# A scratch write behind every row gather in a four-layer graph attention kernel: 320 columns behind each, in place of 256 behind every second

## Chip, cores and metric

The kernel runs on one core of one Trainium2 chip. The metric is the device time of one execution in microseconds. The core's engines are TensorE (PE, with its weight loads shown apart as PEld), VectorE (DVE), ScalarE (ACT), GpSimd (POOL) and SyncE (SP, which issues DMAs).

## What is computed

Four graph attention layers over N = 4096 nodes with 256 features share one adjacency matrix. Each layer normalizes its input, attends along the edges and adds the result to its input:

```
h = maximum(layernorm(x), 0)            # before each layer
x = x + gat_l(h, adj)                   # l = 0..3

# gat_l: h' = h @ W;  s = h' @ a1;  d = h' @ a2
e    = leaky_relu(s[:, None] + d[None, :], 0.2)
attn = softmax(where(adj > 0, e, -big), axis=1)
out  = attn @ h'                        # elu behind it in layers 1 and 3
```

Layer 2 has four heads of 64 columns. Layer 3 has a second attention with -e, and multiplies both results by one matrix. The adjacency is random, and an edge (i, j) is likelier where i and j are small: the first rows are dense, the later ones sparse.

## The kernel before

The nodes are cut into 32 tiles of 128. Blocks of four tiles at the front are computed **densely**: every source tile j is weighed against a 128x512 block of targets (DVE L1151 makes the weights s_p from the target row s_grow, the source's column and the mask) and multiplied on PE (L1193; in layer 2 L1228 and L1210) into accumulators in PSUM. There are 4, 2, 1 and 1 dense blocks in layers 0 to 3. All other target tiles are computed **from lists**. For each of them, the sources that have an edge into it are collected once, in layer 0, in index lists (made with one-hot matmuls L968 and read out into idx at L978). A listed tile T takes the first four source tiles whole, and the others by gathers with an indirect DMA: one gather brings 128 rows of the layer's table in DRAM, named by a column of idx. There are SHARED[T] gathers of rows for the whole tile (s_gg), and QUADS[T] groups of four gathers (s_gq), each of the four for 32 of the targets. That makes 5 to 12 gathers for a tile. In a gathered tile the weights come from L1151 (s_gg) or L1107 and L1110 (s_gq), and L1193 or L1130 multiply them. Where the mask of a tile stands in the same table row, an ACT copy (L1174 for s_gg, L1084 for s_gq) takes it out into mlist for the later layers; masks of the other blocks are gathered in layer 0 by gathers of their own (mlist<-mask_t).

All gathers go through one helper, `gather` (L532), on GpSimd. Behind every second one the helper writes zeros into a scratch tile named pause (L541), which nothing reads. A counter, gathers[0], and the constant RUN = 2 choose after which. GpSimd's order is written out by hand: the whole program of the four layers stands in a manual schedule for that engine, so that what GpSimd does is in the order in which the source emits it. The other engines' orders are set by the framework's scheduler, which reckons with each engine's time. GpSimd's other work is in layer 0: normalization (L732), a bias (L736) and constants.

The order of the work as a whole comes from one plan, a list of steps (unit, i), where a unit is a dense block or a listed tile. `run` goes through it with four stages that stand apart by LEAD = (0, 2, 3, 6) steps: fetch, begin, weigh, multiply. `fetch` is what issues the gathers, six steps ahead of the matmuls that use them. In layer 0 the listed steps are mixed into the later dense blocks; in layers 1 to 3 the dense steps are dealt out over the listed tiles: over 24 tiles in layer 1, over the first 14 in layer 2, and over 26 in layer 3.

The buffers: s_gg has four in layer 0 and six later, s_gq two. A gather waits until the matmuls or weights that used its buffer have run. SP's queue carries the plain loads and stores: the raw adjacency (s_raw<-in_adjT, 128 loads of 512 KB, turned into masks by DVE L1472) in layer 0, the tables' stores, and the streams s_gs and s_ms for the dense blocks.

In time order, layer 0 lasts to about 500 us, layer 1 to about 768, layer 2 to about 1165 and layer 3 to the end. Between layers, GpSimd's first gather waits until the table is complete or a dense start has run: in the trace 58.5 us before layer 1 (the flag that ends layer 0, L1015), 43.1 us before layer 2 (PE L1228) and 30.3 us before layer 3 (the table's store).

Of the kernel before, what the change touches and what calls it, by code (L numbers as in the profile page):

```python
# [8 lines left out]
F32 = mybir.dt.float32  # L9
# [9 lines left out]
P = 128  # L19
# [460 lines left out]
FRONT = tuple(MW * ((l, False) in MASKS_IN.values()) for l in range(4))  # L480
TW = tuple(FRONT[l] + GW[l] + MW * ((l, True) in MASKS_IN.values()) for l in range(4))
LEAD = (0, 2, 3, 6)
RUN = 2
OWN0 = 7
HW = MW // 2
TURNS = (4, 5, 6, 1, 7, 2, 3)
# [3 lines left out]
def list_layers(ctx: ExitStack, tc: tile.TileContext, a: dict, out: bass.AP, flag):  # L490

    nc = tc.nc

    const = ctx.enter_context(tc.tile_pool(name="s_const", bufs=1))
# [29 lines left out]
        nc.gpsimd.memset(places[:, T - TS0 : T - TS0 + 1], float(2 * BASE + P * SHARED[T]))  # L524


    pause = const.tile([P, 256], F32, name="pause")
    gathers = [0]

    def gather(dst, src, index_ap, offset):  # L530

        nc.gpsimd.indirect_dma_start(  # L532
            out=dst,
            out_offset=None,
            in_=src,
            in_offset=bass.IndirectOffsetOnAxis(ap=index_ap, axis=0),
            element_offset=offset,
        )
        gathers[0] += 1
        if gathers[0] % RUN == 0:  # L540
            nc.gpsimd.memset(pause, 0.0)  # L541

    x = keep.tile([P, NT, D], F32, name="x")
    mpre = keep.tile([P, DP, N], U8, name="mpre")
# [452 lines left out]
    def gather_masks(n, tile=None):  # L997

        for T, k in list(masks_of):
            if not n or tile is None and T not in index:  # L1000
                break
            if tile in (None, T):
                slot, c0, c1 = mask_slot(T, k)
                gather(mlist[:, slot, c0:c1], mask_t[T // IT], index[T][:, k : k + 1], T % IT * P + c0)
                masks_of.remove((T, k))
                n -= 1
# [335 lines left out]
    def listed_sources(L, T, pool):  # L1342
# [15 lines left out]
        def gather_rows(dst, k):  # L1358
            gather(dst, source, index[T][:, k : k + 1], first_col - front)
# [306 lines left out]
def gat_layers(tc: tile.TileContext, a: dict, out: bass.AP):  # L1666
    nc = tc.nc
    with tc.tile_pool(name="flag", bufs=1) as pool:
        flag = pool.tile([1, 1], I32, name="flag")

        with tc.manual_schedule(engines={mybir.EngineType.Pool}):
            list_layers(tc, a, out, flag)
        again = nc.values_load(flag[0:1, 0:1], min_val=0, max_val=1)
        with tc.If(again > 0):
            dense_layers(tc, a, out)
# [45 lines left out]
```

## Time and profile before

| | |
|---|---|
| median of 3 runs | 1530.43 us (1529.68 to 1532.2) |
| profiled execution, own time | 1527.76 us |
| its span, first to last instruction | 1526.0 us |
| mean granted TensorE clock | 0.955 |
| PE / DVE / POOL / ACT busy | 1387.2 / 1179.9 / 1061.1 / 499.9 us |
| gathers on POOL | 758: 847.9 us |
| pause on POOL | 379: 132.6 us |
| DMA moved | 272.72 MB, mean 179 GB/s |

The span is what the views of the trace add up to; 1.8 us lie around it. A group in the profile is one line, engine and operation with its count, its busy time in us, the mean of one in ns, and then the idle time of the engine just before these instructions with what ended most of it. A time of POOL for a gather is the time that GpSimd itself is taken, not the transfer. The slices cut the span in 40 parts of 38 us, each digit a busy share in tenths. Idle time of an engine costs nothing unless another waits for it.

### The profile page before, as it was taken

To read this page: it belongs to the slowest core of one execution; us is meant where nothing else is said; L and a number is where in the kernel's file an instruction comes from. 1 tells how busy PE (TensorE), PEld (TensorE's weight loads), DVE (VectorE), ACT (ScalarE), POOL (GpSimd) and SP (SyncE) were. 2 spreads that over 40 slices of the span, in tenths; PEclk is the share of its full clock that TensorE was granted. 3 is DMA by queue.
4 is the path that set the end of the run, shared out by engine and by line. 5 is a ranking of instruction groups with operands and counts; after the bars stand their busy time and mean duration, and the time that the engine had idled before them with its cause. 6 is when DMAs were issued, how large, how long until landed. Compare 5 with 4: busy or idle time off the path is not lost.

```text
span 1526.0 us, 30153 instructions
## 1 busy us (share of the span) xinstructions
PE 1387.2 (91%) x10558; PEld 1051.8 (69%) x10558; DVE 1179.9 (77%) x3424; ACT 499.9 (33%) x1569; POOL 1061.1 (70%) x1255
## 2 busy tenths in 40 slices
PE   5999898989998999987898999999677999999995
PEld 4888676767776877775644655667565887878873
DVE  6979898999887478755598999999776466777764
ACT  5641012112112023332336666578662111111111
POOL 9832888888530578867608878888764588777775
PEclk9999999999998899999999999999888999999997
DMA  7899999997622455555514344345442677777665
GB/s 256 285 321 312 294 306 306 253 240 192 186 63 80 136 143 155 157 155 158 145 51 118 101 121 120 112 122 131 123 131 79 189 221 228 213 206 219 192 180 150
DMA packets 161024, 272.72 MB, mean 179 GB/s; under 512 B 29664, under 2 KB 86462, under 8 KB 160862
## 3 DMA queue, kind: packets, MB, share of 16 engines
q1 hardware_dynamic: 117322, 146.32, 30.8%
q0 software_dynamic: 42704, 123.84, 30.4%
q8 instruction: 86, 1.41, 0.4%
q14 instruction: 76, 0.62, 0.1%
q10 hardware_dynamic: 836, 0.53, 0.1%
HBM read 225.22 MB, written 45.39 MB: 177 GB/s over the span
## 4 chain that ended last, share of the span: by engine, by line
PE 52%; DVE 18%; DMA 11%; POOL 11%; issue 5%; ACT 2%; SPq 0%; POOLq 0%; DVEq 0%; ACTq 0%
PE s_acc L1193 31%; PE s_pj L778 8%; DVE s_p L1151 7%; POOL s_gq L532 5%; DMA s_gq<-table,idx 5%; DMA s_raw<-in_adjT 4%; PE s_acch L1210 3%; PE s_accm L1228 2%; PE s_acc L1130 2%; POOL s_gg L532 2%; DVE s_p L1160 2%; PE idx_ps L968 2%; PE s_tp L746 2%; POOL pause L541 1%; DVE s_m L1472 1%
## 5 line engine op out<-in xcount | busy, mean ns | idle before, releaser
L532 POOL DMA_INDIRECT s_gq<-table,idx x400 | 444.0, 1110 | 121.9 <-issue 83.1
L532 POOL DMA_INDIRECT s_gg<-table,idx x258 | 287.7, 1115 | 229.2 <-DVE bad L1015 58.5
L1193 PE MATMUL s_acc<-g,s_p 128*128 128x257 f32 x1152 | 294.8, 399 | 20.6 <-DVE s_p L1151 20.2
L1193 PEld LDWEIGHTS s_acc<-g,s_p 128*128 128x128 f32 x1152 | 219.0, 199 | 62.9 <-DVE s_p L1151 29.2
L1193 PE MATMUL s_acc<-s_gs,s_p 128*128 128x257 f32 x896 | 214.1, 390 | 0.0
L1151 DVE SCALAR_TENSOR_TENSOR s_p<-s_grow,pre,mpre 128x128 f32<-128x128 f32 (+1 forms) x576 | 188.4, 364 | 29.6 <-PE s_acc L1193 24.6
L778 PE MATMUL s_pj<-s_w,s_hT 128*128 128x259 f32 (+3 forms) x640 | 180.6, 421 | 17.5 <-ACT s_g L813 10.2
L1193 PEld LDWEIGHTS s_acc<-s_gs,s_p 128*128 128x128 f32 x896 | 167.9, 193 | 38.5 <-DVE s_p L1151 5.9
L1193 PE MATMUL s_acc<-pre,s_p 128*128 128x257 f32 x768 | 183.0, 386 | 2.3 <-DVE s_p L1151 1.5
L1151 DVE SCALAR_TENSOR_TENSOR s_p<-s_grow,s_gs,s_ms 128x512 f32<-128x512 f32 x224 | 157.7, 744 | 25.3 <-PE s_acc L1193 19.2
L1193 PEld LDWEIGHTS s_acc<-pre,s_p 128*128 128x128 f32 x768 | 145.0, 193 | 25.9 <-DVE s_p L1151 2.5
L778 PEld LDWEIGHTS s_pj<-s_w,s_hT 128*128 128x128 f32 x640 | 124.3, 205 | 48.1 <-ACT s_hT L748 11.4
L1193 PE MATMUL s_acc<-s_gg,s_p 128*128 128x257 f32 x530 | 136.0, 389 | 2.6 <-DVE s_p L1151 2.5
L532 POOL DMA_INDIRECT mlist<-mask_t,idx x77 | 89.3, 1160 | 65.5 <-DVE idx L978 46.7
L541 POOL MEMSET pause<- 128x256 f32 x379 | 132.6, 350 | 0.2
L1151 DVE SCALAR_TENSOR_TENSOR s_p<-s_grow,s_gg,mlist 128x128 f32<-128x128 f32 x363 | 116.3, 343 | 16.9 <-PE s_acc L1193 16.7
L1107 DVE TENSOR_TENSOR s_p<-s_grow,s_gq 128x128 f32<-128x128 f32 (+1 forms) x168 | 52.1, 337 | 96.5 <-DMA s_gq<-table,idx 61.6
L1042 ACT ACTIVATE s_grow<-s_sT 128x256 f32<-128x256 f32 (+2 forms) x136 | 46.9, 369 | 214.5 <-PE s_sT L1036 211.5
L1193 PEld LDWEIGHTS s_acc<-s_gg,s_p 128*128 128x128 f32 x530 | 100.6, 194 | 18.2 <-DVE s_p L1151 4.2
L1090 ACT ACTIVATE s_p<-s_grow,s_minus,pre 128x128 f32<-128x128 f32 x224 | 96.8, 486 | 39.5 <-PE s_accm L1228 19.6
L1228 PE MATMUL s_accm<-s_p,s_gs 128*65 128x512 f32 x224 | 102.6, 608 | 0.9 <-DVE s_p L1151 0.9
L1472 DVE TENSOR_SCALAR s_m<-s_raw 128x1024 uint8<-128x1024 int32 x112 | 85.6, 775 | 20.9 <-DMA s_raw<-in_adjT 20.7
(154 smaller groups left out, 1980.5 us busy)
## 6 DMA issues: line engine op xcount, KB each, us to landing
s_raw<-in_adjT SPq DMA_DIRECT2D x128, 512.0 KB
s_gs<-table SPq DMA_DIRECT2D x28, 516.0 KB
table<-s_g SPq DMA_DIRECT2D x28, 258.0 KB
mask_t<-s_m SPq DMA_DIRECT2D x28, 256.0 KB
s_ms<-mask_t SPq DMA_DIRECT2D x28, 256.0 KB
s_gq<-table,idx POOLq DMA_INDIRECT x400
table<-s_m SPq DMA_DIRECT2D x21, 256.0 KB
table<-g SPq DMA_DIRECT2D x8, 516.0 KB
```

The lines of the kernel that those rows point to most:

```text
L532: nc.gpsimd.indirect_dma_start(out=dst, out_offset=None, in_=src, in_offset=bass.IndirectOffsetOnAxis(ap=index_ap, axis=0), element_offset ...
L541: nc.gpsimd.memset(pause, 0.0)
L746: nc.tensor.transpose(tp[:, c, :], zs[k][:, c * P : (c + 1) * P], ident)
L778: nc.tensor.matmul(ps, lhsT=hT[:, c, :], rhs=L.w[:, c, k * (D + 6) : k * (D + 6) + cols], start=(c == 0), stop=(c == 1),)
L1042: nc.scalar.activation(grow[:, h1:h2, :], ps[:, h1 - h0 : h2 - h0].rearrange("p h a b -> p h (a b)"), AF.Exp, scale=scale,)
L1090: nc.scalar.activation(w[:, h, :], u.grow[:, h, :], AF.Relu, scale=g[h][:, n - 1 : n], bias=minus)
L1107: nc.vector.tensor_tensor(p4[:, h0:h1], grow[:, h0:h1], c[:, h0:h1].to_broadcast([P, h1 - h0, GR, GP]), op=op)
L1151: nc.vector.scalar_tensor_tensor(p[:, k, :], u.grow[:, h, :], g[k][:, n - 1 : n], m, op0=ALU.min if L.l == 3 and h == 1 else ALU.max, op1= ...
L1193: nc.tensor.matmul(u.accs[it][h], lhsT=p[:, k, it * P : (it + 1) * P], rhs=g[k][:, 0:n], start=first, stop=last, skip_group_check=u.quads > 0,
L1210: nc.tensor.matmul(u.accs[0][c : c + P // 2, h, :], lhsT=p[:, h, c : c + P // 2], rhs=g[h][:, 0 : DH + 1], start=first and h == 0, stop=la ...
L1228: nc.tensor.matmul(u.accs[h], lhsT=g[k][:, 0 : DH + 1], rhs=p[:, k, :], start=first, stop=last, skip_group_check=True,)
L1472: nc.vector.tensor_scalar(m[:, h * half : (h + 1) * half, :], raw, 0.0, None, op0=ALU.is_gt)
```

## The change

The scratch tile grows from 256 to 320 columns, and it is written behind every gather. The counter and RUN go.

```
-RUN = 2
...
-    pause = const.tile([P, 256], F32, name="pause")
-    gathers = [0]
+    pause = const.tile([P, 320], F32, name="pause")
...
             in_offset=bass.IndirectOffsetOnAxis(ap=index_ap, axis=0),
             element_offset=offset,
         )
-        gathers[0] += 1
-        if gathers[0] % RUN == 0:
-            nc.gpsimd.memset(pause, 0.0)
+        nc.gpsimd.memset(pause, 0.0)
```

There are 758 gathers in the program before and after, in the same order on GpSimd.

## The prediction

> **What bounds the kernel now.** I read the page first. It shows four engines busy at once, none at its limit: PE 91% of the span, DVE 77%, POOL 70%. The slices show that the shares are not spread evenly.
>
> ```profile
> PE   5999898989998999987898999999677999999995
> POOL 9832888888530578867608878888764588777775
> L532 POOL DMA_INDIRECT s_gq<-table,idx x400 | 444.0, 1110 | 121.9 <-issue 83.1
> L532 POOL DMA_INDIRECT s_gg<-table,idx x258 | 287.7, 1115 | 229.2 <-DVE bad L1015 58.5
> L532 POOL DMA_INDIRECT mlist<-mask_t,idx x77 | 89.3, 1160 | 65.5 <-DVE idx L978 46.7
> L541 POOL MEMSET pause<- 128x256 f32 x379 | 132.6, 350 | 0.2
> ```
>
> POOL is at 8 tenths over long stretches. Its work there is gathers (400 + 258 + 77 + 16 + 7 = 758 with those from table_own) and 379 pauses. The idle "issue" before a gather is no wait for anyone: it is the time between two instructions. The timeline shows how it falls (start, duration, idle before in brackets):
>
> ```profile
> 1481.31 0.95 POOL L532 DMA_INDIRECT s_gq<-table,idx  x1 [0.31 <-issue]
> 1482.26 0.33 POOL L541 MEMSET pause<- 128x256 f32 x1
> 1482.75 0.95 POOL L532 DMA_INDIRECT s_gg<-table,idx  x1 [0.17 <-issue]
> 1484.00 0.95 POOL L532 DMA_INDIRECT s_gg<-table,idx  x1 [0.31 <-issue]
> 1484.95 0.33 POOL L541 MEMSET pause<- 128x256 f32 x1
> 1485.13 0.49 DVE L1107 TENSOR_TENSOR s_p<-s_grow,s_gq 128x128 f32<-128x128 f32 x2 [3.89 <-DMA s_gq<-table,idx]
> ```
>
> A gather behind a gather starts 0.31 us after it; a pause starts at once, and the gather behind it 0.17 us later. POOL is never free here, and DVE waits 3.89 us for rows that POOL has just asked for. Next the windows by stage, all engines (length, then busy us of PE, PEld, DVE, ACT, POOL; clock; DMA share; GB/s):
>
> ```profile
> 200.00:400.00 200.00, 182.98 (x1128) 147.25 (x1127) 181.44 (x482) 33.84 (x123) 159.59 (x179) 0.96 0.92 251
> 680.00:768.00 88.00, 74.48 (x366) 56.79 (x365) 50.57 (x149) 27.19 (x96) 60.90 (x81) 0.94 0.53 147
> 808.00:1100.00 292.00, 274.19 (x3859) 175.26 (x3854) 272.45 (x862) 197.43 (x558) 248.40 (x248) 0.98 0.43 118
> 1210.00:1470.00 260.00, 256.88 (x1451) 206.02 (x1450) 184.41 (x576) 39.21 (x100) 199.98 (x255) 0.99 0.72 209
> 1470.00:1526.00 56.00, 35.59 (x242) 25.44 (x241) 27.78 (x96) 8.26 (x22) 32.85 (x42) 0.84 0.57 159
> ```
>
> and the chain of waits for the end of layer 2 (1100 to 1165) and of layer 3 (1470 to 1526):
>
> ```profile
> by line: POOL s_gq L532 25.6%; DMA s_gq<-table,idx 21.3%; issue 14.3%; PE s_pj L778 5.5%; DMA s_gg<-table,idx 5.4%; ACT s_p L1090 4.9%; POOL pause L541 3.5%; DVE s_p L1151 3.0%; DVE s_z L732 2.4%; PE s_acch L1130 2.4%; DVE s_p L1107 2.3%; D
> by line: POOL s_gq L532 28.9%; DMA s_gq<-table,idx 21.7%; issue 10.3%; PE s_acc L1130 5.4%; POOL pause L541 4.7%; POOL s_gg L532 3.4%; DVE s_p L1151 3.3%; DVE s_p L1107 2.6%; DVE s_p L1110 1.4%; DVE s_out L1269 1.4%; DVE s_y L1318 0.9%; PE
> ```
>
> In the middle of a layer PE or DVE sets the pace with POOL close behind. At the ends, where little dense work is left, half the chain and more is gathers, pauses and landings. In 680 to 768, the end of layer 1, the same chain has POOL at 27% and landings at 16%.
>
> **What the Trainium skill says.** "SBUF — State Buffer", section "Who interferes with whom": a DVE instruction with two SBUF inputs contends with a GpSimd instruction that reads SBUF, not with one that only writes it. The trace fits: from 800 to 1100, where DVE's two-input work fills 93%, the pause keeps 325/330/359 ns (shortest, median, longest), while gathers, which read the index from SBUF, go from 942 to 5016 ns with a mean of 221.6/166 = 1.33 us. So a longer pause is not stretched by this work, but the gathers are, and less so when DVE stands idle. "Perfetto Trace Analysis", section "DMA Instruction — SWDGE (GPSIMD)": the end of such an instruction is the end of descriptor writing, not of the data. Above, the last s_gq gather ends at 1482.26 and DVE starts on it at 1485.13, 2.9 us later. A pause behind a gather therefore doesn't delay that gather's data, only the gathers queued after it.
>
> **The change part by part.** The 379 pauses of 256 columns go; 758 of 320 columns come. The trace has no 320-column write; it has 128x128 f32 at 195 to 205 ns and 256 columns at 330, 1.0 ns a column, so I take 330 + 64 = 0.395 us. Per pair of gathers, before: 0.305 between the two, then 0.330 + 0.165, together 0.80. After: 2 x (0.395 + 0.165) = 1.12. Each gather costs POOL **0.16 us** more; 758 of them make 121 us. No semaphore wait is added on the other engines. A pause waits only for the pause before it. Queued behind it are the next gathers, POOL's order being written by hand and unchanged otherwise; for their rows wait ACT (mask copies L1084, L1174), DVE (L1107, L1151) and through them PE. SP's order is unchanged; the scheduler moves a few dozen DVE and ACT instructions and a handful of PE ones by a few places, which I cost at nothing (bounds -2 to +2 us). What counts is how far POOL's own waits absorb the 0.16 us:
>
> - Layer 0, 139 to 400: 157 gathers, +25 us. POOL waits 10.8 us once for idx (L978) at 397. The stage is led by raw loads (15% of its chain from 200 to 400, gathers 5% and their landings 4%). I take +6, bounds -15 to +20. The 24 gathers from 400 to 500 are covered: POOL is busy 30 of 100 us.
> - Layer 1, 500 to 768: POOL fills its buffers, waits 15.2 us for PE until 535.7, and from there on waits only 2.8 + 6.0 + 1.0 = 9.8 us. About 150 gathers follow: 24 - 9.8 = **+14**, bounds 7 (end alone: 54 x 0.16 = 8.6) to 24.
> - Layer 2, 808 to 1100: 166 gathers, +26.6, POOL's true waits 1.2 + 3.2 + 1.1 = 5.5, so +21 if gathers stay at 1.33 us. But POOL late means DVE idle, and a gather without DVE in its way takes 0.95. I take about half, **+12**, bounds 0 and 24.
> - Layer 2, 1100 to 1165: 37 gathers, on the chain: 5.9, less a little of one wait of 8.7 for PE, **+5**, bounds 2 and 6.
> - Layer 3, 1210 to 1526: 198 gathers, +31.7. Waits for PE before 1470 are 16.3 + 13.8 us in 37 pieces, of which 37 x 0.235 is plain issue: some 21 absorb. **+11**, bounds 4.5 (the 28 gathers of the end) and 30.
> - The 18 gathers from 768 to 808 and 1165 to 1210: nothing, since POOL waits over 40 us for PE and 30.3 for table<-s_g. If that cover failed, 2.9 us.
>
> Sum 6 + 14 + 12 + 5 + 11 = 48 us. The profiled execution took 1527.76 us (span 1526.0 and 1.8 around it); that gives 1575.8. The median of the runs, 1530.43, is 2.7 higher, so the forecast is **1578 us**.
>
> **Rivals.** A measurement of this kernel can tell about 0.2%, 3 us, from no change.
>
> Mostly hidden: the middle of each layer absorbs all, and only the ends count, 8.6 + 4 + 4.5 = 17 us: 1547. For it: PE has 257 of 260 us in layer 3's middle and POOL waits for it there. Against it: layer 2 has POOL without waits for 292 us.
>
> POOL paces all: nothing absorbs, 757 x 0.16 = 121 us less what the starts cover, some 80 to 110: 1610 to 1640. For it: POOL's rare waits in layers 1 and 2. Against it: 21 us of waits in layer 3, and shorter gathers once DVE idles.
>
> Faster: thinner gathers let the raw loads through in layer 0. The skill's "DMA: Bandwidth & Descriptors", section "Issuing engines are not separate DMA queues", says that all queues share the 16 DMA engines; the trace has them 92% busy from 200 to 400. POOL has 64 idle us from 400 to 500, where the DMA share is 0.32, so gathers pushed there cost nothing. DVE's L1472 waits 20.7 us in all for s_raw: that is the price that could come back. It decides only if the later layers also hide their 0.16 us, about 10 us earlier than now: 1520. Against it: gathers at the ends of layers 1 to 3 are on the chain and there are no raw loads.
>
> That the pause is not written as told is excluded: the built program has 758 writes of 128x320 on POOL.
>
> **How the numbers follow.** The forecast's partial absorption 0.62; mostly hidden 0.12; POOL paces all 0.12; faster 0.10; the gain of layer 0 and the loss at the ends cancel, 0.04. Slower is 0.62 + 0.12 + 0.12 = 0.86, same 0.04, faster 0.10. The forecast's own bounds, taken together at half their depth, are 1550 to 1610. The range goes on to 1540 below, into the hidden case, and to 1622 above, into the lower half of the full one. Left out are no change, faster, and the top: under 2 in 10.
>
> **What would show it.** Right: a pause at 0.39 us, x758, some 295 to 310 us in all; POOL near 1220 us busy; gathers all with 0.17 before them; the stretches of POOL's waits for PE in layer 3 gone; DVE L1107's waits for s_gq longer; layer 2's mean gather shorter than 1.33 us; the excess in layers 1 to 3, not in layer 0. Wrong: a layer that ends as early as before though POOL is 10% busier in it, gathers that shrink by as much as the pauses grow, or raw-load waits that fall by more than 10 us.

## The result

The changed kernel takes 1592.99 us (median of 4 runs, 1591.85 to 1597.29) against 1530.06 us before (4 runs, 1522.49 to 1532.2): a ratio of 1.0433, 95% interval 1.0401 to 1.0465, **slower by 4.3%**. The forecast was 1578 with a range of 1540 to 1622. The profiled execution took 1592.9 us, its span 1591.2 against 1526.0. Six of the experiment runs below (e5 to e8, e11, e12) were timed on two other chips than the other six; there the kernel before took 1645.33 and 1666.63 us itself.

The page after, the lines that answer to those shown of before (slices, then groups; a slice is now 39.8 us, and line numbers have moved by two to four):

```profile
PE   5999888879988998977888999999977999999985
POOL 9823999989650578888826999899885588888885
L530 POOL DMA_INDIRECT s_gq<-table,idx x400 | 445.1, 1113 | 73.3 <-issue 61.4
L530 POOL DMA_INDIRECT s_gg<-table,idx x258 | 278.1, 1078 | 198.0 <-DVE bad L1011 58.0
L537 POOL MEMSET pause<- 128x320 f32 x758 | 300.5, 396 | 0.5
L530 POOL DMA_INDIRECT mlist<-mask_t,idx x77 | 83.8, 1088 | 61.7 <-DVE idx L974 49.2
```

POOL is at 9 tenths where it was at 8. Its share of the span went from 70% to 76%, PE's from 91% to 88%. Pauses went from 132.6 to 300.5 us; a gather of s_gq takes as long as before in the mean, those of s_gg and of the masks a little less. The timeline near the end of layer 3, as before:

```profile
1543.36 0.95 POOL L530 DMA_INDIRECT s_gq<-table,idx  x1 [0.17 <-issue]
1544.32 0.38 POOL L537 MEMSET pause<- 128x320 f32 x1
1544.86 0.95 POOL L530 DMA_INDIRECT s_gg<-table,idx  x1 [0.16 <-issue]
...
1547.11 0.49 DVE L1103 TENSOR_TENSOR s_p<-s_grow,s_gq 128x128 f32<-128x128 f32 x2 [4.46 <-DMA s_gq<-table,idx]
```

A gather now comes every 1.50 us; before, two came in 2.69 (from 1482.75 to 1485.44), 1.35 each.

The windows of the same five stages, each moved to where its first gather now stands, with the columns as in the prediction:

```profile
206.00:427.00 221.00, 190.89 (x1122) 150.88 (x1123) 192.07 (x486) 33.61 (x122) 189.90 (x241) 0.91 0.82 223
720.00:817.00 97.00, 78.00 (x378) 59.70 (x378) 53.69 (x161) 26.75 (x97) 75.60 (x110) 0.93 0.49 135
857.00:1153.00 296.00, 276.73 (x3832) 177.03 (x3828) 275.44 (x861) 197.12 (x555) 267.28 (x325) 0.95 0.43 114
1264.00:1532.00 268.00, 260.96 (x1462) 207.37 (x1464) 184.63 (x577) 39.19 (x100) 236.76 (x340) 0.98 0.71 204
1532.00:1591.00 59.00, 36.45 (x236) 25.81 (x228) 26.74 (x94) 8.32 (x22) 39.12 (x56) 0.82 0.55 151
```

Layer 0's stage grew most, by 21 of 200 us, with PE, DVE and ACT running nearly the same number of instructions. The chain of waits within it, first before (200 to 400 us), then after (206 to 427 us), now names POOL where it named the raw loads:

```profile
by line: PE s_acc L1193 17.4%; DMA s_raw<-in_adjT 15.0%; issue 10.5%; PE idx_ps L968 4.9%; DVE s_p L1151 4.9%; POOL s_gq L532 4.7%; DMA table<-s_g 4.3%; DMA s_gq<-table,idx 4.0%; DVE s_m L1472 4.0%; PE s_pj L778 3.3%; DMA mlist<-mask_t,idx 
by line: PE s_acc L1189 13.1%; POOL s_gq L530 12.3%; POOL pause L537 10.1%; issue 10.1%; POOL mlist L530 6.6%; DMA s_gq<-table,idx 6.0%; POOL s_gg L530 5.4%; DVE s_m L1468 4.8%; DVE s_p L1147 4.7%; DMA s_gg<-table,idx 4.1%; PE idx_ps L964 4
```

Gathers and pauses of POOL together are 34% of it (12.3 + 10.1 + 6.6 + 5.4).

Layer by layer the excess is this. A layer's end is read from the trace: layer 0 ends with the first gather of layer 1, the one that waits for the flag (DVE bad); layer 1 with the first matmul of layer 2 (PE s_accm); layer 2 with its last one (PE s_acch).

| profiled execution, us | layer 0 | layer 1 | layer 2 | layer 3 | span |
|---|---|---|---|---|---|
| before | 498.2 | 270.0 | 402.0 | 355.8 | 1526.0 |
| after | 525.5 | 291.4 | 406.8 | 367.5 | 1591.2 |
| more | 27.3 | 21.4 | 4.8 | 11.7 | 65.2 |
| forecast | 6 | 14 | 17 | 11 | 48 |

PE's granted clock fell from 0.955 to 0.942 in the mean, and the same 10558 matmuls kept PE busy for 1404.7 us in place of 1387.2. The clock goes with the time in the experiments too: 0.963 in e3 and 0.930 in e10. No run holds it fixed, so it is not shown whether the lower clock adds a part of the 65 us by itself.

### The profile page after: what moved, and what is told of

It is laid out like the page before. It is cut to its first block, busy times and chain, and to the rows that moved or that the text cites. A ratio compares the mean times of both kernels' runs of the same rounds, so it can differ in the third digit from the quotient of the medians.

```text
span 1591.2 us, 30529 instructions
## 1 busy us (share of the span) xinstructions
PE 1404.7 (88%) x10558; PEld 1059.8 (67%) x10558; DVE 1190.2 (75%) x3424; ACT 499.2 (31%) x1569; POOL 1214.6 (76%) x1634
## 3 DMA queue, kind: packets, MB, share of 16 engines
q0 software_dynamic: 42704, 123.84, 29.8%
## 4 chain that ended last, share of the span: by engine, by line
PE 44%; POOL 25%; DVE 14%; DMA 10%; issue 5%; ACT 1%; POOLq 0%; DVEq 0%; SPq 0%; ACTq 0%
PE s_acc L1189 24%; POOL s_gq L530 10%; PE s_pj L774 7%; POOL pause L537 6%; DMA s_gq<-table,idx 6%; POOL s_gg L530 5%; DVE s_p L1147 4%; PE s_accm L1224 3%; PE s_acch L1206 3%; PE s_acc L1126 2%; POOL mlist L530 2%; DMA s_gg<-table,idx 2%; PE idx_ps L964 1%; DVE s_m L1468 1%; PE s_sT L1032 1%
## 5 line engine op out<-in xcount | busy, mean ns | idle before, releaser
L530 POOL DMA_INDIRECT s_gg<-table,idx x258 | 278.1, 1078 | 198.0 <-DVE bad L1011 58.0
L537 POOL MEMSET pause<- 128x320 f32 x758 | 300.5, 396 | 0.5
L1189 PE MATMUL s_acc<-s_gg,s_p 128*128 128x257 f32 x530 | 132.7, 383 | 2.2 <-DVE s_p L1147 2.2
L530 POOL DMA_INDIRECT mlist<-mask_t,idx x77 | 83.8, 1088 | 61.7 <-DVE idx L974 49.2
L1126 PE MATMUL s_acc<-s_gq,s_p 128*32 128x257 f32 x832 | 64.9, 416 | 42.3 <-DVE s_p L1106 42.3
```

Source lines behind the costliest of these rows:

```text
L530: nc.gpsimd.indirect_dma_start(out=dst, out_offset=None, in_=src, in_offset=bass.IndirectOffsetOnAxis(ap=index_ap, axis=0), element_offset ...
L1126: nc.tensor.matmul(acc, lhsT=p[:, h, part], rhs=g[:, k, h * n : (h + 1) * n - 1], start=False, stop=last, skip_group_check=True,)
L1189: nc.tensor.matmul(u.accs[it][h], lhsT=p[:, k, it * P : (it + 1) * P], rhs=g[k][:, 0:n], start=first, stop=last, skip_group_check=u.quads > 0,
```

## The experiments

Each starts from the kernel before. Their layers, read in the same way, in us:

| kernel | layer 0 | layer 1 | layer 2 | layer 3 | span |
|---|---|---|---|---|---|
| e1_size_only | 497.7 | 276.1 | 399.3 | 356.8 | 1529.9 |
| e2_count_only | 515.3 | 288.6 | 408.8 | 363.3 | 1576.0 |
| e3_no_pause | 483.7 | 271.5 | 392.9 | 349.2 | 1497.3 |
| e4_layer0_only | 526.3 | 270.3 | 396.9 | 350.8 | 1544.3 |
| e9_one_column | 488.9 | 271.1 | 396.2 | 348.3 | 1504.5 |
| e10_layer2_twice | 494.2 | 273.3 | 484.4 | 354.4 | 1606.3 |

Where nothing was changed, layers differ between these kernels and the one before: layer 2 by 5.1 us and layer 3 by 5.0 in e4, layer 0 by 4.0 in e10. A layer's difference under some 5 us says nothing.

**Size alone, count alone.** In e1 the tile has 320 columns, and RUN stays 2. In e2 it has 256, and the write stands behind every gather:

```
e1:  pause = const.tile([P, 320], F32, name="pause")    # gathers[0] % RUN as before
e2:  pause = const.tile([P, 256], F32, name="pause")
     ...
     nc.gpsimd.memset(pause, 0.0)                       # behind every gather
```

> Only the size of the pause changes: 320 columns, still behind every second gather, 379 in all. Theory A (POOL's time per gather is what is paid): a gather costs POOL (0.305 + 0.395 + 0.165)/2 = 0.4325 us of gap and pause in place of 0.40; at the rate that the change showed (63 us for 0.16 us more per gather) that is +13 us, about 1543, spread over layers 0, 1 and 3. Rival B (the number of writes is paid, each one costing POOL a switch, whatever its length): no change within 3 us. Rival C (the scheduler's new order of DVE, ACT and PE instructions is what is paid): unclear sign, within 10 us, since only some 10 instructions move.

Measured: 1535.6 us against 1524.17, ratio 1.0084 (1.0054 to 1.0114), 11.4 us more.

> Only the count changes: 256 columns, behind every gather, 758 in all. Theory A: 0.330 + 0.165 = 0.495 us per gather in place of 0.40, so 63 x 0.095/0.16 = +37 us, about 1567. Rival B: nearly all of the change, +55 to +63 us, about 1590. Rival C: PE's order is that of the kernel before, some 20 DVE instructions move; if the order paid, less than +10 us.

Measured: 1575.43 us, ratio 1.0323 (1.0287 to 1.0359), 51 us more than the 1524.17 of before (49 by the ratio). The size alone costs about what theory A said. Where it is paid doesn't show: the profiled execution was the fastest of e1's runs, and only layer 1 is longer there by more than 5 us. The count alone costs more than A's 37 and less than rival B's 55 to 63. PE's order in e2 is that of before, so rival C falls for PE; e4 below leaves the order of all three engines as it was and still pays. A had spread the change's cost evenly over its time on POOL. The table shows that it isn't even: layers 0 and 1 give 17.1 and 18.6 us of e2's excess, layers 2 and 3 together 14.3.

**No pause, and a pause of one column.** e3 leaves the write out. e9 writes one column behind every gather, so it keeps all 758 writes and nearly none of their length:

```
e9:  pause = const.tile([P, 1], F32, name="pause")
     ...
     nc.gpsimd.memset(pause, 0.0)                       # behind every gather
```

> No pause at all. Theory A: 0.305 us per gather in place of 0.40; at the same rate -37 us, but PE and DVE, 91% and 77% busy, take over where POOL stops leading, so -15 to -37, 1493 to 1515. Rival B: 379 writes fewer, as many as the change added, -50 to -63. Rival D (the pauses protect something, such as DVE's turn at a shared port or the raw loads' turn on the DMA engines, and gathers without them get longer): gathers of 1.2 us and more in the mean, and a time no better than before, 1525 to 1560.

Measured: 1504.29 us, ratio 0.9873 (0.9836 to 0.991), 20 us faster than before. In the profiled execution layers 0, 2 and 3 are 14.5, 9.1 and 6.6 us shorter; layer 1 is not shorter at all.

> The pause shrunk to one column of 128 partitions, behind every gather. The profiles before show a gather 0.305 us behind another gather and 0.165 us behind a pause, and one-column writes elsewhere at 0.09 to 0.10 us. Theory A (POOL's time per gather): 0.10 + 0.165 = 0.265 us per gather, less than the 0.305 with no pause at all; 758 x 0.04 = 30 us less of POOL than without pauses, of which a quarter to a half is paid (removing all pauses took 0.105 us per gather, 80 us, and gave 19): 7 to 15 us faster than the kernel without pauses, 1487 to 1500 if the kernel before stands at 1524. Rival B (each write costs a switch of its own, of some 0.1 us and more, beside its length): no faster than without pauses, 1504 or slower, up to 1540.

Measured in e5_one_column: 1706.13 us against 1645.33, ratio 1.0272 (1.0167 to 1.0376), on one of the two other chips. Its trace has PE waiting for nothing but "issue" ahead of s_acch for 29.8 us in 53 places, which the profile of before doesn't show at all. The same kernel was run again as e9, on the chip of e1 to e4:

> The one-column pause behind every gather again, since the run e5_one_column fell into a time in which the kernel before itself took 1645 us and PE stood idle for its own instructions. Measured there: the one-column write takes 0.113 to 0.117 us and the gather starts 0.19 us behind it, so 0.305 us per gather, just the gap of two gathers without a pause. Theory A (POOL's time per gather): the same as without pauses, 19 us faster than before, within 6. Rival B (each write costs something beside its time on POOL): slower than without pauses by 10 us or more, so no more than 10 us faster than before.

Measured: 1504.8 us against 1525.17, ratio 0.9868 (0.9832 to 0.9903). With 758 writes the kernel is as fast as with none. Rival B falls: a write costs its time on POOL and nothing else that these runs can tell. The timeline of e9 shows why the two are equal, not one faster than the other as the first expectation had it:

```profile
701.39 0.12 POOL L538 MEMSET pause<- 128x1 f32 x1
701.70 0.94 POOL L531 DMA_INDIRECT s_gg<-table,idx  x1 [0.19 <-issue]
702.63 0.12 POOL L538 MEMSET pause<- 128x1 f32 x1
```

0.12 and 0.19 us make the 0.31 that lie between two gathers anyway. Rival D falls too on this chip: without pauses the gathers' means are 1076 ns (s_gq) and 1105 (s_gg) against 1110 and 1115. Nothing was protected by the pauses in these two runs, and both versions are faster than the kernel before and the one after. For layer 2 on the other chips, e6 and e12 below show something else.

**Layer 0 alone.** e4 has the change for the gathers of layer 0, and 256 columns behind every second gather in the others:

```
         gathers[0] += 1
-        if gathers[0] % RUN == 0:
+        if first_layer[0]:
             nc.gpsimd.memset(pause, 0.0)
+        elif gathers[0] % RUN == 0:
+            nc.gpsimd.memset(pause[:, 0:256], 0.0)
```

> The change in layer 0 alone: 320 columns behind each of its gathers; in layers 1 to 3 256 columns behind every second one as before. The order on PE, DVE and ACT is exactly that of the kernel before. Theory A, with layer 0 led by POOL although its chain named the raw loads: about 157 gathers x 0.16 = +25 us, 1555, all of it before 527 us, and layers 1 to 3 as long as before. Rival (layer 0's +27 us in the changed kernel came from elsewhere, or my +6 was right when the later layers are left alone): 1530 to 1538.

Measured: 1547.93 us against 1524.17, ratio 1.0154 (1.012 to 1.0189), +23.8 us. Layer 0 takes 526.3 us, as in the changed kernel. The rival falls: layer 0 pays all of its 157 x 0.15. What POOL waits for in e4 between 200 and 430 us:

```profile
POOL s_gg L533 <- DVE idx L981: 9.6, 1, 9.6
```

The wait for idx is still there, 9.6 us in place of 10.8, though POOL ends its last write ahead of it at 414.2 us in place of 386.6. So it wasn't slack: what POOL waits for was late with POOL. The lists for idx are made by PE and DVE from the masks of the raw loads, and these are late as well. DVE's conversion of the last one (s_m), which comes after this wait, starts at 455.4 us in e4, at 454.5 in the changed kernel and at 427.8 before. Which step hands the lateness on to the lists is not shown.

**Layer 2 with two writes behind each gather.** e6 and e12 put one write of 320 columns behind each of layer 2's gathers, e7 and e10 two:

```
e10:     if src is table[2]:
             nc.gpsimd.memset(pause, 0.0)
             nc.gpsimd.memset(pause, 0.0)               # once in e6 and e12
         elif gathers[0] % RUN == 0:
             nc.gpsimd.memset(pause[:, 0:256], 0.0)
```

> As the run with 320 columns in layer 2 alone, with two such writes behind each gather of layer 2: about 0.57 us more per gather than before, 118 us in all. Theory (the cover is the stretch of the gathers and POOL's small waits, and it can be used up): gathers can shorten to 0.96 us at the least, 0.33 x 204 = 67 us, and POOL's own waits in layer 2 hold some 6, so 118 - 73 = +45 us or more, up to +75 if the gathers keep a part of the stretch. Rival (a fixed share of about a third is paid, whatever the dose): +30 to +40.

Measured in e7_layer2_twice: 1663.47 us against 1645.33, ratio 1.0202 (1.0121 to 1.0282), on the chip of e5. Again as e10, on the chip of e9:

> Two writes of 320 columns behind each gather of layer 2 again, for the same reason. About 0.57 us more per gather, 118 us in all. Theory (cover is the stretch of layer 2's gathers and can be used up): gathers of layer 2 at 1.0 to 1.1 us in the mean, and +45 to +75 us. Rival (a fixed share of about a third): +30 to +40.

Measured: 1608.22 us against 1525.17, ratio 1.0553 (1.0513 to 1.0593), +83 us, above both. The windows over the whole of layer 2, all engines, of the kernel before, of the one after and of e10, with the columns as above:

```profile
804.00:1171.00 367.00, 324.23 (x4719) 212.20 (x4718) 318.66 (x1018) 237.87 (x679) 296.73 (x308) 0.94 0.44 119
```
```profile
853.00:1224.00 371.00, 328.49 (x4718) 215.53 (x4715) 321.45 (x1016) 237.74 (x679) 326.86 (x410) 0.92 0.44 118
```
```profile
804.00:1252.00 448.00, 351.29 (x4719) 228.23 (x4717) 322.44 (x1019) 238.37 (x679) 373.86 (x618) 0.86 0.35 98
```

and POOL's time for the gathers alone in the same windows (length, busy us, count, clock, DMA share, GB/s):

```profile
804.00:1171.00 367.00, 263.02 (x205) 0.94 0.44 119
```
```profile
853.00:1224.00 371.00, 248.37 (x205) 0.92 0.44 118
```
```profile
804.00:1252.00 448.00, 218.83 (x206) 0.86 0.35 98
```

The same gathers (205 in a window, 206 in the last) take POOL 263.0, 248.4 and 218.8 us, that is 1.28, 1.21 and 1.06 each, while DVE, whose work is the same, fills 87%, 87% and 72% of the time. DVE's share fits the step to e10, but not the one from before to after, where it doesn't change. Gather by gather the trace of before does show a link: of layer 2's 208 gathers, the 173 beside which DVE was busy for over nine tenths of the time took 1.32 us in the mean, and the 22 beside which it was busy for less than half took 0.97. In e10 the gathers gave 44 us back and still POOL was 77 us busier; the layer became 82 us longer. The cover exists, as the theory had it, but against a large dose it is some 36 us (118 - 82), not the theory's 73. e6 and e12 were to say what the single dose costs; both came to run on the other chips.

> 320 columns behind each gather of layer 2 alone (208 gathers); elsewhere 256 columns behind every second one. Theory (gathers of layer 2 stand in DVE's way less when POOL is late, so part of the 208 x 0.15 = 31 us is taken back): gathers of layer 2 shorten from a mean of 1.29 to about 1.2 us, and the kernel is 5 to 12 us slower. Rival (POOL paces layer 2 in full, as it does layers 0 and 1): 25 to 31 us slower, gathers as long as before.

Measured in e6_layer2_320: 1607.19 us against 1645.33, ratio 0.9701 (0.9642 to 0.976).

> 320 columns behind each gather of layer 2 alone, again, since the run e6_layer2_320 was disturbed. 204 gathers x 0.15 = 31 us more of POOL. The double write took 0.57 x 204 = 117 us of POOL and cost 83. Theory (about 35 us of cover in layer 2, in the gathers' stretch and DVE's lead, that the first dose nearly fits into): +5 to +12 us, gathers of layer 2 at 1.2 us in the mean. Rival (the same share for each dose, 83/117 = 0.7): +20 to +25.

Measured in e12_layer2_320: 1627.55 us against 1666.63, ratio 0.981 (0.9761 to 0.9859). A kernel that only adds to POOL comes out faster there than the one before. The layers of these traces, read as in the table, say where. Layer 2 takes 472.4 us in e8 and 468.9 in e11, the two runs below that leave this layer as it was. With the single dose it takes 435.9 in e6, on the chip of e8, and 444.1 in e12, on that of e11. PE's waits for "issue" ahead of s_acch go down as well, here from e8 to e6 and likewise from 34.8 us in e11 to 15.6 in e12:

```profile
PE s_acch L1212 <- issue: 32.4, 72, 1.1
PE s_acch L1212 <- issue: 9.9, 29, 0.5
```

With two writes (e7) these waits are 0.7 us, and layer 2 takes 485.7 us, nearly the 484.4 of e10. So on these two chips longer writes shorten layer 2 by 25 to 36 us, up to some dose, and rival D is not refuted there. Why PE's matmuls come late in these places, and whether it is the chip or the hour that makes the difference, no run shows. The whole change was not timed where the kernel before takes 1645 us or more. Where it takes 1524, the price of the single dose by itself stays open; only the whole change shows it, with 4.8 us for layer 2.

**The masks' gathers alone.** e8 and e11 put 320 columns behind each of the 77 gathers of masks in layer 0 (`if src in mask_t.values()` in e4's place).

> In layer 0, 320 columns behind each of the 77 gathers of masks (mlist), whose data later work needs, and 256 columns behind every second one of all the others. The order on PE, DVE and ACT is exactly that of the kernel before. Theory (in layer 0 it is POOL's throughput that is paid, so it doesn't matter behind which gather the time is put): half of what all of layer 0's writes cost (23.5 us for 157 gathers), so +10 to +13. Rival (what is paid is the late landing of the rows that the next matmuls wait for): 0 to +4.

Measured in e8_masks_only: 1634.58 us against 1645.33, ratio 0.9929 (0.9895 to 0.9964).

> 320 columns behind each of layer 0's 77 gathers of masks, again, since the run e8_masks_only was disturbed. Theory (POOL's throughput paces layer 0, whichever gather is followed by the write): about half of the 23.5 us that the writes behind all of layer 0's gathers cost, +10 to +13 us. Rival (only the late landing of rows that the next matmuls wait for is paid): 0 to +4.

Measured in e11_masks_only: 1653.02 us against 1666.63, ratio 0.9919 (0.9888 to 0.995). e8 ran on the chip of e6, e11 on that of e12. Neither theory expected a gain. Layer 0, where the writes were added, takes 510.3 us in e8 against 523.6 in e6, which leaves that layer as it was, but 518.2 in e11 against 512.2 in e12. The two pairs disagree in sign, so the theories are not told apart. Whether it matters in layer 0 behind which gather the time is put stays open.

## Why the prediction was right or wrong

**The time on POOL: right.** The pause takes 396 ns in the mean where 395 was worked out, 758 of them 300.5 us (295 to 310 expected), and a gather that waits for nothing has 0.17 us before it. POOL is 1214.6 us busy (near 1220). That the mean fits so well is partly luck: in layers 1 to 3 a write takes 0.381 to 0.385 us, less than the price, and in layer 0 it takes 0.440, because 23 of its 177 take 0.5 to 0.9 us, 22 of these while DVE converts a raw load. Per gather, with the means of both pages, the cost went from (0.305 + 0.350 + 0.165)/2 = 0.41 to 0.396 + 0.165 = 0.56: 0.15 us more, where the prediction had 0.16.

**Direction and mechanism: right.** e9 against e2, with 758 writes in both, shows that it is the length of the writes that is paid, and e4 that it is paid with the other engines' order unchanged. The mechanism leaves out what e6 and e12 show, a layer 2 that gets shorter with longer writes on the other chips.

**Layer 0: wrong, the step "I take +6, bounds -15 to +20".** It cost 27.3 us, and e4 shows 23.8 on its own. Two readings failed. POOL's wait of 10.8 us for idx was counted as a place where lateness is lost; it moved along with the lateness (9.6 in e4, 9.8 after). And the chain with 15% raw loads was read as loads that lead, when POOL had hardly another wait from 200 to 386 us (2.7 us for PE, with the gaps in it). The chain goes back through what released each step last; it doesn't say what would have to be quicker. That the loads themselves were late because the plan asks for them step by step behind the listed tiles is how I read the code; no run took that apart.

**Layer 1: too small, the step "24 - 9.8 = +14".** It cost 21.4. Of the waits that were to absorb, here is the one for the projection (s_hT) before, and then what is left after the change (total, times, longest):

```profile
POOL s_gg L532 <- ACT s_hT L748: 7.1, 2, 6.0
...
POOL s_gg L530 <- ACT s_hT L744: 5.3, 1, 5.3
...
POOL s_gg L530 <- PE s_acc L1126: 2.2, 3, 1.8
```

The 6.0 us for the projection are still 5.3, so that wait wasn't slack either. The 2.8 for PE is gone, but one of 1.8 is new, at an earlier gather. The prediction's reading had also left out two waits for PE, of 1.4 and 1.3 us. In all, POOL's waits behind the first fill of its buffers went from 12.5 us to 8.2. Some 4 us were absorbed in place of 9.8, and 24 - 4 is 20 of the 21.4.

**Layer 2: too large, the steps "+12" and "+5".** It cost 4.8, within what layers differ by in themselves. Its gathers were expected to shorten from 1.33 us in the middle, and they did, to 1.26; over the whole layer they went from 1.28 to 1.21, 15 us in all. POOL's idle time in the windows fell from 367 - 296.7 = 70.3 to 371 - 326.9 = 44.1 us. Of that, 102 gaps of 0.305 became 0.165, 14 us, and the other 12 were waits. So 31 us more of writes and gaps met 15 + 12 us of cover. The starts of the gathers say where. From 807.7 to 1101.2 us before, which is 857.4 to 1159.3 after, POOL fell behind by 8.5 us more, where +12 was forecast. The next gather has the one wait of 8.7 us for PE, from which the prediction took only "a little", first before, then after:

```profile
1110.86 1.03 POOL L532 DMA_INDIRECT s_gq<-table,idx  x1 [8.73 <-PE s_acch L1130]
1163.89 0.95 POOL L530 DMA_INDIRECT s_gq<-table,idx  x1 [3.12 <-PE s_acch L1126]
```

POOL is 58.1 us late at the gather ahead of it, 53.0 at this one and 54.7 at the layer's last. So the end gave back 3.4 us where +5 was forecast: this wait was slack, though the chain of the layer's end had POOL on it.

**Layer 3: right.** 11.7 us against 11. POOL's waits for PE in its middle, 16.3 and 13.8 us before, are nearly gone, as foretold; two lines of before, two of after:

```profile
POOL s_gq L532 <- PE s_acc L1130: 16.3, 9, 3.2
POOL s_gg L532 <- PE s_acc L1193: 13.8, 28, 1.9
POOL s_gg L530 <- PE s_acc L1189: 2.6, 16, 0.2
POOL s_gq L530 <- PE s_acc L1126: 1.7, 2, 1.2
```

What is left is nearly only the plain 0.17 before a gather. These were true slack: PE was full, and buffers came free at PE's pace.

**The rivals.** "Mostly hidden" and "faster" fell. DVE's waits for raw loads did fall in layer 0, from 20.7 us to 14.2, but by less than the 10 us named, and its waits for s_gq rose there from 2.9 to 23.3. "POOL paces all" comes near in layers 0 and 1 alone, with 27.3 and 21.4 us for 25 and 24. The statement of the Trainium skill's "SBUF — State Buffer", section "Who interferes with whom", that a write alone doesn't meet DVE's two-input work agrees with layer 2, where the pauses' mean is 0.385 us, as in layers 1 and 3 (0.383 and 0.381). That the gathers' stretch in layer 2 comes from the contention named there is argued from their lengths beside a busy and an idle DVE; no run took DVE's work away.

The sum was 48 for 65 because layer 0 was given slack and had none (+21), layer 1 had less than it was given (+7), and layer 2, which was thought to pay half, paid a seventh (-12). That the forecast of 1578 is only 15 us from the 1593 measured is in part luck: without their signs the layers' misses make some 42 us.

## What to carry to other kernels

An engine's idle time absorbs a delay only if what it waits for doesn't depend on that engine: follow each wait to its source before it is subtracted. Here, waits for buffers that a busier engine frees were slack (layer 3, and the one of 8.7 us in layer 2). Waits for data that came late together with the engine were not (idx in layer 0, s_hT in layer 1). Where an engine shows only its plain issue gaps over a long stretch, don't take its added time off because the chain names another: layer 0 paid all of it. But ask whether its own instructions can get shorter, as the gathers in layer 2 did. And a price of a few per cent that was found on one chip can have another sign on the next.

## What the runs showed of the hardware

A write of 0.12 us between two gathers was free on GpSimd: gather to gather leaves 0.305 us, a one-column write of 0.12 leaves 0.19 behind it, and 1504.8 us in the whole is the same as 1504.29 with no write. From 256 to 320 columns a write grew by 0.05 us where it isn't stretched (0.33 to 0.38 in the timelines), less than the 1.0 ns a column that was inferred from 128 and 256 columns. And a gather's time on GpSimd isn't a constant: in layer 2 it went from 1.28 to 1.06 us as DVE's share fell from 87% to 72%, and within one trace from 1.32 us beside a busy DVE to 0.97 beside a mostly idle one. The same kernel took 1524 us on one chip and 1645 and 1667 on two others, in medians.
